# Reordering the first slice's sums, the stores of adj x, and the weight and feature loads of the first layer

## The chip, the cores and the metric

The kernel runs on one core of one Trainium2 chip, in one launch. The metric is the device time in microseconds (us). Three runs of the kernel before gave 1675.24, 1675.89 and 1678.59 us; their median is 1675.89 us.

## The reference

Four layers work on x of shape (8 batches, 2048 nodes, 64 features) with one dense adjacency matrix of 2048 x 2048, all in fp32. Each layer is `x = layernorm(x + f(x))` over the 64 features:

- layer 0: three Chebyshev terms x, A x and 2 A (A x) - x, each multiplied by weights of its own for every node (node embedding of 16 numbers times a weight bank of 16 x 3 x 64 x 64), plus a bias per node;
- layer 1: twice `relu((A x) W)`;
- layer 2: `x W_self + (A x) W_neighbor + b`;
- layer 3: x, A x, 2 A A x - x (twice, with the same matrix), concatenated and projected.

What takes the time is seven products of A with a 2048 x 512 matrix (all batches and features side by side) and the per-node projection of layer 0.

## The kernel before

**Fast products.** A product A b is computed by Strassen-Winograd on two levels: seven products of matrix halves instead of eight, A11, A12, A22, S1, S2, S3, S4, and each of these again as seven products of quarters. Left-hand sums such as S1 = A21 + A22 are made once, while A is first read, and stored in HBM as `comb` tensors; right-hand sums are made on VectorE (DVE) at each product.

**First product, by slices (L627 to L1005).** A x for layer 0 runs in four column slices, `ns` = 0 to 3. A slice is four chunks of 1 MB, `chunks[ns, j]`, loaded on the SyncE (SP) queue into a ring of four tiles (`slice_chunk`, L153) in the order j = 2, 3, 0, 1 (`AHEAD`). While TensorE (PE) multiplies a slice, the generator `prepare` (L627) makes the left-hand sums from the same chunks on DVE. Outer sums S1, S2, S4, S3 (`outer`, L657) go into tiles with the tag T, of which there are three; inner sums of four quarters each (`inner`, L644) go into tiles with the tag C, of which there are four. Each sum is stored to `comb` by GpSimd's DMA queue (POOL, `keep`, L640). All DVE instructions of `prepare` carry `keep_in_program_order`, so the places of its `yield`s fix the DVE order. Slice 0 is multiplied plainly in part (`plain_slice`, L846) and slices 1 to 3 by `fast_slice` (L880). In slice 1 the first inner sums that PE reads are those of A22, in a small two-level product (`two_level`, L802; matmuls of L816), and its chunks 0 and 1 are first read by the matmuls of L902 that make `pa` (L940).

**Queue of SP around slice 0.** After slice 0 the program issues the small weights (`load_weights`, L990), the four chunks of slice 1 (L991) and then the stores of adj x, transposed, to `t1T` (`keep_t1`, L767, called at L996). These instructions carry no fixed order, so the scheduler places them by its own estimate of when they are ready: in the kernel before, two chunks of slice 1, four stores, then six chunks. [...] a chunk's load waits until PE and DVE have read the tile it overwrites.

**Second product and the per-node projection (L1023 to L1097).** `product(1, ...)` (L212) goes through A11, S1, A12, S2, S4, S3, A22. Each takes seven loads of 1 MB (`load`, L196) into the same ring of four tiles, and each load feeds one group of eight matmuls (L273). A load is issued when PE has finished with the load four before it. Into this queue the kernel before also puts the loads of `xT` and `tT` for the projection (`fetch`, L1048): `tT` reads back what `keep_t1` stored. The projection's weights `wn` (1.5 MB) come on the POOL queue in two DMAs of 768 KB (L1032). `sum_wn` (L1034) combines and centers them in eight DVE instructions right after S1 (argument `between`, L419). The projection itself is `feature0` (L1055, matmuls of L1071), a job of a list (`pump`) that runs when `pump.run` is called: with `RUNS = {S2: NP, S3: NP}` four jobs after S2 and four after S3; the others run where all jobs are drained.

Of the kernel before, what the change touches and what calls it, by code (L numbers as in the profile page):

```python
# [11 lines left out]
ALU = mybir.AluOpType  # L12
# [6 lines left out]
GW = 512  # L19
# [3 lines left out]
A11, A12, A22, S1, S2, S3, S4 = range(7)  # L23
# [81 lines left out]
def kernel(  # L105
# [18 lines left out]
    nc = tc.nc  # L124
# [3 lines left out]
    F = b_l0.shape[1]  # L128
# [3 lines left out]
    NP = B // 2  # L132
    DH = D // 2
    RING = 4
# [10 lines left out]
    pump = Pump()  # L145
# [44 lines left out]


    loads = 0
    banks = 0
    p_mm2 = None

    def load(q, s):  # L196
        nonlocal loads
        loads += 1
        turn = loads % (RING + 3)
        pool = ring2 if ring2 is not None and turn >= RING else ring  # L200
        a = pool.tile([P, TG, TG, P], F32, tag="a", name="a")
        if q in (A11, A12, A22) and s < 4:
            i, j = {A11: (0, 0), A12: (0, 2), A22: (2, 2)}[q]
            fetched = nc.sync.dma_start(a, blocks[i + s // 2, j + s % 2])
        else:
            fetched = nc.sync.dma_start(a, comb[q][s].rearrange("p (n m c) -> p n m c", n=TG, m=TG))
        if ring2 is not None and loads <= RING + 3:

            tc.keep_in_program_order(fetched)
        return a  # L210

    def product(src, feature, between=None, rate=1, own=None, pin=False, runs=None, onto_slot=None, ends=False):  # L212
# [251 lines left out]
    class Norm:  # L464
# [18 lines left out]
        def center(self):  # L483
            sm = self.new("sm")
            nc.vector.tensor_reduce(sm, self.v, AX.X, ALU.add)
            nc.vector.scalar_tensor_tensor(self.v, self.wide(sm), -1.0 / F, self.v, ALU.mult, ALU.add)
# [91 lines left out]
    if True:  # L578
# [48 lines left out]
        def prepare(ns, ch, outers):  # L627

            ch = [c.rearrange("p m i n -> p i m n") for c in ch]

            def add(out, a, b, op=ALU.add):

                tc.keep_in_program_order(nc.vector.tensor_tensor(out, a, b, op))

            def kept(tag, shape, bufs):
                s = sums.tile([P, *shape, GW], F32, tag=tag, name="s" + ("i" if tag == "C" else "o"), bufs=bufs)
                n = "ab"[: len(shape)]
                return s, s.rearrange(f"p {' '.join(n)} (m n) -> p {' '.join(n)} m n", m=TG)

            def keep(q, s0, src):  # L640
                dst = comb[q][s0 : s0 + src.shape[1]].rearrange("s p (n c) -> p s n c", n=TG)
                nc.gpsimd.dma_start(dst[:, :, ns], src)

            def inner(q, q00, q01, q10, q11):  # L644
                flat, s = kept("C", (4,), 4)
                add(s[:, 0], q10, q11)
                add(s[:, 1], s[:, 0], q00, ALU.subtract)
                add(s[:, 2], q00, q10, ALU.subtract)
                add(s[:, 3], q01, s[:, 1], ALU.subtract)
                if q is not None:  # L650
                    keep(q, 4, flat)
                return flat

            def raw(I, J):
                return [ch[2 * J + b][:, 2 * I + a] for a in range(2) for b in range(2)]

            def outer(a, b, op):  # L657

                flat, s = kept("T", (2, 2), 3)
                for c in range(2):  # L660
                    add(s[:, :, c], a(c), b(c), op)
                return flat

            def rq(I, J):
                return lambda c: ch[2 * J + c][:, 2 * I : 2 * I + 2]

            def sq(s):
                return lambda c: s[:, :, c].rearrange("p a (m n) -> p a m n", m=TG)

            def put(q, s):  # L670
                flat = s.rearrange("p a b c -> p (a b) c")
                keep(q, 0, flat[:, :2])
                keep(q, 3, flat[:, 3:])
                inner(q, *(flat[:, k].rearrange("p (m n) -> p m n", m=TG) for k in range(4)))


            outers[A22] = inner(A22, *raw(1, 1))
            yield
            inner(A12, *raw(0, 1))
            if ns == 0:  # L680

                sums_of_blocks()
                outers[A11] = inner(A11, *raw(0, 0))
                outers[A21] = inner(None, *raw(1, 0))
            outers[S1] = s1 = outer(rq(1, 0), rq(1, 1), ALU.add)
            outers[S2] = s2 = outer(sq(s1), rq(0, 0), ALU.subtract)
            outers[S4] = s4 = outer(rq(0, 1), sq(s2), ALU.subtract)
            yield
            put(S1, s1)
            yield  # L690
            put(S2, s2)
            if ns:
                inner(A11, *raw(0, 0))
            yield
            outers[S3] = s3 = outer(rq(0, 0), rq(1, 0), ALU.subtract)
            yield
            put(S3, s3)
            put(S4, s4)
            yield

        with tc.tile_pool(name="p_n", bufs=4, space=PSUM) as p_n, tc.tile_pool(
# [63 lines left out]
                return p_n.tile([P, GW], F32, tag="mm", name="ps_n")  # L765

            def keep_t1(ns, p, hT):  # L767
                nc.sync.dma_start(
                    t1T[p].rearrange("f (i n c) -> f i n c", i=NG, n=TG)[:, :, ns],
                    hT.rearrange("f (i c) -> f i c", i=NG),  # L770
                )

            def new_h():
                return sums.tile([P, GW], F32, tag="t", name="hT", bufs=5)
# [195 lines left out]
            for ns in range(TG):  # L970
                ch = [chunks.pop((ns, j)) for j in range(NG)]
                if ns == 0:
                    outers = {}
# [50 lines left out]
        if True:  # L1024
# [3 lines left out]
            nc.gpsimd.dma_start(e_sb, emb)  # L1028

            wn = l0y.tile([P, 3, D, F], F32, tag="wn", name="wn")  # L1030
            for k in range(2):
                nc.gpsimd.dma_start(wn[k * F : (k + 1) * F], w_l0.rearrange("n i d o -> i n d o"))  # L1032

            def sum_wn():  # L1034
                pin = tc.keep_in_program_order
                pin(nc.vector.tensor_tensor(wn[:, 0], wn[:, 0], wn[:, 2], ALU.subtract))
                pin(nc.vector.tensor_scalar(wn[:, 2], wn[:, 2], 2.0, None, ALU.mult))
                for n in range(3):
                    center(wn[:, n], pin=pin)


            order = [
# [2 lines left out]
            ]  # L1045
            fetched = {}

            def fetch(k):  # L1048
                if k < len(order):
                    i, p = order[k]  # L1050
                    fetched[i, p] = [l0y.tile([P, GW], F32, tag=n, name=n, bufs=2) for n in ("xT", "tT")]
                    for tile_, src in zip(fetched[i, p], (xT, t1T)):
                        nc.sync.dma_start(tile_, src[p][:, ts(i, GW)])

            def feature0(g, p, hT):  # L1055
                if (g, p) == order[0]:
                    fetch(0)
                fetch(order.index((g, p)) + 1)
                terms = fetched.pop((g, p)) + [hT]
                for k in range(TG):  # L1060
                    t = g * TG + k
                    acc = xy[:, t, 0, ts(p, 2 * F)].rearrange("p (b f) -> p b f", f=F)


                    s = l0y.tile([P, DH, 2, F], F32, tag="s", name="s", bufs=2)
                    for h in range(2):
                        y = p_y.tile([P, 2, DH * F], F32, tag="y", name="y")
                        for n in range(3):
                            for b in range(2):
                                half = slice(b * F, (b + 1) * F)  # L1070
                                mm = nc.tensor.matmul(  # L1071
                                    y[:, b, :], terms[n][half, ts(k, P)],
                                    wn[half, n, h * DH : (h + 1) * DH, :],
                                    start=(n == 0), stop=(n == 2),
                                )
                                if n == b == h == 0:
                                    tc.keep_in_program_order(mm)
                        for d in range(DH):
                            e = e_sb[:, t, h * DH + d : h * DH + d + 1]
                            if h == 0:  # L1080
                                nc.vector.scalar_tensor_tensor(  # L1081
                                    acc, y[:, :, ts(d, F)], e, acc, ALU.mult, ALU.add
                                )
                            else:
                                nc.scalar.activation(s[:, d], y[:, :, ts(d, F)], AF.Copy, scale=e)  # L1085
                        if h == 0:
                            yield
                    n = DH // 2
                    while n:
                        nc.gpsimd.tensor_tensor(s[:, :n], s[:, :n], s[:, n : 2 * n], ALU.add)  # L1090
                        n //= 2
                    nc.gpsimd.tensor_tensor(acc, acc, s[:, 0], ALU.add)
                    yield


            RUNS = {S2: NP, S3: NP}
            product(1, then(feature0, 0, gap=4, pool_sq=True), sum_wn, rate=4, runs=RUNS)  # L1097


    late = p_z = None  # L1100
# [127 lines left out]
```

## Time and profile before

| what | value |
|---|---|
| median of three runs | 1675.89 us |
| the profiled execution's own time | 1674.71 us |
| its span, first to last instruction | 1672.9 us |
| around the span (difference) | 1.81 us |
| PE busy | 1657.7 us, 99% of the span |
| PE weight loads (beside PE) | 1061.1 us, 63% |
| DVE busy | 965.5 us, 58% |
| ScalarE (ACT) busy | 275.6 us, 16% |
| POOL busy | 246.9 us, 15% |
| mean granted PE clock | 0.997 |
| loads of A blocks and sums (`a<-comb`, `a<-in_blocks`) | 294 of 1 MB, median 4.8 us from issue to landing |
| chunks of slices (`a<-in_slices`, 1 MB) | 15, median 10.3 us to landing |
| stores `t1T<-hT` | 16 of 256 KB, median 6.5 us |
| `wn` on the POOL queue | 2 of 768 KB, median 16.9 us |

The profile is one execution. A page lists the busy time of each engine, the span in 40 slices of 41.8 us with the granted PE clock and the share of the 16 DMA engines, the chain of work that ended last, and groups of instructions by line. Other views of the same trace are used below: the waits by engine, the timeline of one engine in a window, and busy times by window. Times in them are microseconds from the start of the span. In a timeline line the columns are start, length, engine, line, operation, tiles, number of instructions, and in brackets the idle time ahead of it with what ended it. A line that merges several DMA issues covers the stretch from the first issue to the end of the last, waits included.

### The profile page before, as it was taken

To read this page: it belongs to the slowest core of one execution; us is meant where nothing else is said; L and a number is where in the kernel's file an instruction comes from. 1 tells how busy PE (TensorE), PEld (TensorE's weight loads), DVE (VectorE), ACT (ScalarE), POOL (GpSimd) and SP (SyncE) were. 2 spreads that over 40 slices of the span, in tenths; PEclk is the share of its full clock that TensorE was granted. 3 is DMA by queue.
4 is the path that set the end of the run, shared out by engine and by line. 5 is a ranking of instruction groups with operands and counts; after the bars stand their busy time and mean duration, and the time that the engine had idled before them with its cause. 6 is when DMAs were issued, how large, how long until landed. Compare 5 with 4: busy or idle time off the path is not lost.

```text
span 1672.9 us, 21268 instructions
## 1 busy us (share of the span) xinstructions
PE 1657.7 (99%) x8414; PEld 1061.1 (63%) x8414; DVE 965.5 (58%) x1737; ACT 275.6 (16%) x811; POOL 246.9 (15%) x334
## 2 busy tenths in 40 slices
PE   9999989999999999999999999999999999999998
PEld 5898844444444444444454455589998455569998
DVE  5986886457456456654434365873568344443657
ACT  0200100143143044430010011120001011100001
POOL 1221200155055056660000000000000000000000
PEclk9999999999999999999999999999999999999999
DMA  8899898503702800009877876667888866678995
GB/s 317 294 395 339 307 321 308 210 26 127 251 26 87 290 26 26 26 31 371 292 261 276 303 275 239 239 223 257 294 292 298 306 219 228 229 268 292 316 314 166
DMA packets 82436, 391.57 MB, mean 234 GB/s; under 512 B 8897, under 2 KB 25537, under 8 KB 42785
## 3 DMA queue, kind: packets, MB, share of 16 engines
q1 hardware_dynamic: 69104, 345.20, 58.5%
q0 software_dynamic: 11664, 43.65, 6.9%
q8 instruction: 67, 1.10, 0.3%
q10 hardware_dynamic: 1568, 1.35, 0.3%
q14 instruction: 33, 0.26, 0.0%
HBM read 339.85 MB, written 50.33 MB: 233 GB/s over the span
## 4 chain that ended last, share of the span: by engine, by line
PE 98%; DMA 2%; DVE 0%; issue 0%; SPq 0%; DVEq 0%
PE y L1071 20%; PE mmb L273 17%; PE mmc L273 12%; PE mma L273 11%; PE mmb L266 9%; PE ps_n L902 7%; PE mma L266 6%; PE mmc L266 6%; PE z L1123 3%; PE ps_i L816 2%; PE z L1152 2%; PE ps_n L856 2%; PE pt L1114 1%; DMA t1T<-hT 1%; DMA a<-in_slices 1%; DMA a<-comb 0%
## 5 line engine op out<-in xcount | busy, mean ns | idle before, releaser
L273 PE MATMUL mmb<-a,t 128*128 128x512 f32 x648 | 292.0, 593 | 0.0
L1081 DVE SCALAR_TENSOR_TENSOR xy<-y,e_sb,xy 128x128 f32<-128x128 f32 x512 | 179.6, 351 | 141.2 <-PE y L1071 125.3
L273 PEld LDWEIGHTS mmb<-a,t 128*128 128x128 f32 x648 | 121.7, 190 | 145.0 <-issue 143.5
L1090 POOL TENSOR_TENSOR s<-s 128x512 f32<-128x512 f32 (+2 forms) x192 | 157.1, 818 | 340.3 <-ACT s L1085 330.1
L1085 ACT ACTIVATE s<-y,e_sb 128x128 f32<-128x128 f32 x512 | 138.9, 382 | 231.9 <-PE y L1071 231.9
L224 DVE TENSOR_TENSOR u<-mmb,p 128x512 f32<-128x512 f32 x84 | 57.8, 688 | 177.5 <-PE mmb L273 121.1
L266 PE MATMUL mmb<-t,a 128*128 128x128 f32 x1344 | 157.0, 275 | 0.0
L266 PEld LDWEIGHTS mmb<-t,a 128*128 128x128 f32 x1344 | 153.5, 192 | 0.0
L1071 PE MATMUL y<-wn,xT 64*128 64x512 f32 x512 | 131.6, 591 | 0.0
L1071 PE MATMUL y<-wn,tT 64*128 64x512 f32 x512 | 131.2, 589 | 0.0
L1071 PE MATMUL y<-wn,C 64*128 64x512 f32 x512 | 131.2, 589 | 0.0
L273 PE MATMUL mma<-a,T 128*128 128x512 f32 x256 | 115.5, 594 | 0.0
L273 PE MATMUL mmc<-a,t 128*128 128x512 f32 x216 | 97.3, 593 | 0.0
L288 ACT COPY p<-mma 128x512 f32<-128x512 f32 x42 | 24.6, 586 | 411.9 <-PE mma L273 270.4
L1071 PEld LDWEIGHTS y<-wn,xT 64*128 64x128 f32 x512 | 49.4, 187 | 61.1 <-issue 60.6
L1071 PEld LDWEIGHTS y<-wn,tT 64*128 64x128 f32 x512 | 49.7, 187 | 60.2 <-issue 60.2
L1071 PEld LDWEIGHTS y<-wn,C 64*128 64x128 f32 x512 | 49.7, 187 | 60.2 <-issue 60.2
L273 PE MATMUL mma<-a,xy 128*128 128x512 f32 x192 | 86.7, 594 | 0.0
L273 PEld LDWEIGHTS mma<-a,T 128*128 128x128 f32 x256 | 47.7, 191 | 56.7 <-issue 56.4
L224 DVE TENSOR_TENSOR C<-mmc,C 128x512 f32<-128x512 f32 x48 | 33.2, 691 | 85.3 <-PE mmc L273 74.5
L273 PEld LDWEIGHTS mmc<-a,t 128*128 128x128 f32 x216 | 40.1, 191 | 45.4 <-issue 45.1
L1123 PEld LDWEIGHTS z<-wd,C 128*128 128x128 f32 x384 | 50.2, 192 | 21.7 <-issue 20.8
(157 smaller groups left out, 2115.3 us busy)
## 6 DMA issues: line engine op xcount, KB each, us to landing
a<-comb SPq DMA_DIRECT2D x240, 1024.0 KB, 4.8
a<-in_blocks SPq DMA_DIRECT2D x54, 1024.0 KB, 4.8
comb<-si POOLq DMA_DIRECT2D x28, 1024.0 KB, 9.8
a<-in_slices SPq DMA_DIRECT2D x15, 1024.0 KB, 10.3
comb<-so POOLq DMA_DIRECT2D x16, 512.0 KB, 11.6
comb<-so POOLq DMA_DIRECT2D x16, 256.0 KB, 11.4
t1T<-hT SPq DMA_DIRECT2D x16, 256.0 KB, 6.5
xT<-in_xT SPq DMA_DIRECT2D x16, 256.0 KB, 3.4
```

The lines of the kernel that those rows point to most:

```text
L224: nc.vector.tensor_tensor(out, a, b, op)
L266: nc.tensor.matmul(to, a[:, k, m, :], xb[:, m, :], start=(start and opens and m == 0), stop=(m == TG - 1), skip_group_check=True,)
L273: nc.tensor.matmul(ps, xb[:, m, :], a[:, :, m, :], start=(start and m == 0), stop=(m == TG - 1), skip_group_check=True,)
L816: nc.tensor.matmul(ps, x[:, m // 2, m % 2], s[n](m), start=(start and m == 0), stop=(m == TG - 1), skip_group_check=True,)
L856: mm = nc.tensor.matmul(ps[p], xcol(0, TG * j + m, p), ch[j][:, m], start=(n == 0 and m == 0), stop=(n == 1 and m == TG - 1), skip_group_c ...
L902: nc.tensor.matmul(ps[:, ts(p, GW // 2)], b(k, p), a(k // TG, k % TG), start=(start and p == k == 0), stop=(k == NT // 2 - 1), skip_group_ ...
L1071: mm = nc.tensor.matmul(y[:, b, :], terms[n][half, ts(k, P)], wn[half, n, h * DH : (h + 1) * DH, :], start=(n == 0), stop=(n == 2),)
L1081: nc.vector.scalar_tensor_tensor(acc, y[:, :, ts(d, F)], e, acc, ALU.mult, ALU.add)
L1085: nc.scalar.activation(s[:, d], y[:, :, ts(d, F)], AF.Copy, scale=e)
L1090: nc.gpsimd.tensor_tensor(s[:, :n], s[:, :n], s[:, n : 2 * n], ALU.add)
L1123: nc.tensor.matmul(z[:, k, :], aT[:, ts(k, P)], wd[:, w, :], start=(n == 0), stop=(n == len(terms) - 1),)
L1152: nc.tensor.matmul(z[n][:, k], xT[half, ts(k, P)], w[half], start=True, stop=True)
```

## The change

- **Third outer sum of slice 0.** S3 of slice 0 is made right after S4, ahead of the first `yield` that follows, in a tile of tag C instead of T. Its inner sums (`put(S3)`) then take the place where S3 itself was made. Slices 1 to 3 are as before.
- **Stores of slice 0.** The four `t1T` stores of slice 0 keep their program order, behind the four chunk loads of slice 1.
- **Weights `wn`.** Six DMAs of 256 KB on the SP queue, two for each of the three terms in the order 0, 2, 1, replace the two DMAs of 768 KB on POOL. `load` issues one behind its 6th, 9th, 12th, 15th, 18th and 21st load, in program order.
- **`sum_wn`.** It becomes a job of `pump`, the first one, and runs after A12 instead of after S1.
- **First `xT` and `tT`.** The first two pairs keep their program order: the first `feature0`, which runs after S2, issues both. In the built order they stand behind S2's last load.

In the built order of the changed kernel the instructions of PE and ACT are in the same order as before. On DVE, besides what is named, three sums of slice 1 (L924, L957, L958 of the kernel before) stand some ten small instructions later among the weight sums.

```diff
+    pieces = []
...
     def load(q, s):
...
+        if pieces and loads > RING and loads % 3 == 0:
+            tc.keep_in_program_order(pieces.pop(0)())
         return a
...
-            def outer(a, b, op):
-                flat, s = kept("T", (2, 2), 3)
+            def outer(a, b, op, tag="T"):
+                flat, s = kept(tag, (2, 2), 3 if tag == "T" else 4)
...
             outers[S4] = s4 = outer(rq(0, 1), sq(s2), ALU.subtract)
+            if ns == 0:
+                s3 = outer(rq(0, 0), rq(1, 0), ALU.subtract, "C")
             yield
             put(S1, s1)
             yield
             put(S2, s2)
             if ns:
                 inner(A11, *raw(0, 0))
             yield
-            outers[S3] = s3 = outer(rq(0, 0), rq(1, 0), ALU.subtract)
-            yield
+            if ns:
+                outers[S3] = s3 = outer(rq(0, 0), rq(1, 0), ALU.subtract)
+                yield
             put(S3, s3)
+            if ns == 0:
+                yield
             put(S4, s4)
...
             def keep_t1(ns, p, hT):
-                nc.sync.dma_start(
+                stored = nc.sync.dma_start(
...
+                if ns == 0:
+                    tc.keep_in_program_order(stored)
...
-            for k in range(2):
-                nc.gpsimd.dma_start(wn[k * F : (k + 1) * F], w_l0.rearrange("n i d o -> i n d o"))
+            pieces += [
+                lambda k=k, n=n: nc.sync.dma_start(wn[k * F : (k + 1) * F, n], w_l0[n])
+                for n in (0, 2, 1) for k in range(2)
+            ]
...
-            def fetch(k):
+            def fetch(k, pin=lambda inst: inst):
...
-                        nc.sync.dma_start(tile_, src[p][:, ts(i, GW)])
+                        pin(nc.sync.dma_start(tile_, src[p][:, ts(i, GW)]))
...
                 if (g, p) == order[0]:
-                    fetch(0)
-                fetch(order.index((g, p)) + 1)
+                    fetch(0, tc.keep_in_program_order)
+                    fetch(1, tc.keep_in_program_order)
+                else:
+                    fetch(order.index((g, p)) + 1)
...
-            RUNS = {S2: NP, S3: NP}
-            product(1, then(feature0, 0, gap=4, pool_sq=True), sum_wn, rate=4, runs=RUNS)
+            RUNS = {A12: 1, S2: NP, S3: NP}
+            product(1, then(feature0, 0, gap=4, pool_sq=True), lambda: pump.add(sum_wn()), rate=4, runs=RUNS)
```

More of the change, by code (lines that the diff above doesn't have):

```diff
@@ L1039, in sum_wn @@
                     center(wn[:, n], pin=pin)
+                yield
             order = [
```

## Prediction

> **What bounds the kernel now.** I read the page's busy slices first, then PE's waits, then the timelines of PE, SP and DVE around each wait.
>
> ```profile
> PE   9999989999999999999999999999999999999998
> ...
> PEclk9999999999999999999999999999999999999999
> DMA  8899898503702800009877876667888866678995
> ```
>
> PE is over 90% busy in 38 of 40 slices, at full clock; only the sixth (209 to 251 us) and the last show less. So a gain can come only from PE's waits. They are few:
>
> ```profile
> PE mmc L273 <- DMA a<-comb: 5.5, 1, 5.5
> PE ps_n L902 <- DMA a<-in_slices: 1.7, 1, 1.7
> PE rise L711 <- DVE zero L708: 1.1, 1, 1.1
> PE pt_n L458 <- ACT xy L459: 0.3, 1, 0.3
> ```
>
> The first two are near the edits; the start (1.1 us) and the chain behind the last matmul (the rest of the 15.2 us in which PE is idle) are untouched. Wait B, in the second product, on PE:
>
> ```profile
> 223.44 3.60 PE L273 MATMUL mmb<-a,C 128*128 128x512 f32 x8
> 232.56 5.40 PE L273 MATMUL mmc<-a,C 128*128 128x512 f32 x8 [5.53 <-DMA a<-comb]
> 237.80 3.60 PE L273 MATMUL mmb<-a,C 128*128 128x512 f32 x8
> ```
>
> Groups follow each other every 3.43 us (216.57, 220.00, 223.44). Unheld, this one begins at 226.87 and the next at 230.30, not 237.80: B costs 7.50 us, of which some 1.8 us is the group that ran 5.40 instead of 3.60 us. On SP, before it:
>
> ```profile
> 211.06 7.87 SPq L768 DMA_DIRECT2D t1T<-hT  x4
> 223.88 0.81 SPq L1053 DMA_DIRECT2D tT<-t1T  x2
> 224.79 0.38 SPq L206 DMA_DIRECT2D a<-comb  x1
> ```
>
> The load that PE waits for stands behind the two tT loads, and these wait for the stores that they read back to land (the chain gives 12.76 us from 211.06). It then needs 7.64 us. Wait A, in slice 1:
>
> ```profile
> 68.23 1.10 PE L816 MATMUL ps_i<-si,t 128*128 128x128 f32 x8
> ...
> 73.64 1.89 PE L902 MATMUL ps_n<-a,xy 128*128 128x256 f32 x8
> 77.23 2.00 PE L902 MATMUL ps_n<-a,xy 128*128 128x256 f32 x8 [1.70 <-DMA a<-in_slices]
> ```
>
> The second eight would follow 1.79 us after the first, at 75.43: A costs 1.80 us. Chunk 1 of slice 1 is issued at 66.66, behind the stores of slice 0, and lands at 77.19. DVE meanwhile:
>
> ```profile
> 40.15 0.55 DVE L831 TENSOR_TENSOR u<-u,part 128x384 f32<-128x384 f32 x1
> ...
> 63.44 2.35 DVE L633 TENSOR_TENSOR so<-a 128x1024 f32<-128x1024 f32 x2
> 65.71 0.69 DVE L633 TENSOR_TENSOR si<-a 128x512 f32<-128x512 f32 x1
> 66.43 0.69 DVE L633 TENSOR_TENSOR si<-si,a 128x512 f32<-128x512 f32 x1
> ```
>
> DVE is without a pause from 40 to 66 us (12.66 of 13.00 us busy between 53 and 66). The pair at 63.44 is S3 of slice 0; the lines after it are A22's inner sums of slice 1, of which PE reads the second at 68.23.
>
> [...] behind 5.53 us of idling the granted clock is 0.69 from 233 to 238 us, behind 1.70 us it is 1.00. [...] from 211 to 220 us POOL's queue takes 76.5% of the engines and SP's 27.0%, so SP's stores are slow while POOL's `comb` stores and `wn` drain. [...]
>
> **The change part by part.**
>
> *xT and tT behind S2's loads.* Load 5 of the second product then stands behind the four stores only. Its tile is free when group 1 ends (216.6); the stores are issued by 218.93 (211.06 + 7.87). So it is issued at 216.7 to 219.0 and lands, at its own 7.64 us, at 226.6 at worst; at the median of 4.8 us, at 221.5. PE wants it at 226.87. B goes, with the slow group: **-7.50 us**, at worst 0.1 to 1 us left. The two pairs now are issued when S2's third group has been read: 303.04 in the old time. They land 3.4 us later and the projection begins at 316.86: 10 us of cover. What is late next? DVE in A11 has, laid end to end from 227.7, the sum that frees the bank of S1's first group done 0.9 us before that group begins; nothing is late.
>
> *wn in six pieces on SP.* POOL loses two issues of 0.63 us. 1.5 MB and the two xT (0.5 MB) leave the crowded stretch 197 to 224 us, where SP's and POOL's transfers took up to 18 us to land; this is why I take the early end for load 5. The pieces then stand between loads 6 and 21. A load is issued three groups (10.3 us) before use and lands in 4.8: slack 5.5 us. A piece takes 256 KB by 385 GB/s (the rate from 230 to 240 us) = 0.68 us. From 238 to 260 us the engines are 0.86 busy at 302 GB/s; 1.5 MB in 56 us add 28 GB/s: 0.94. Cost 0; if the slack were gone, 0.7 us each, 4 us in all. What waits behind a piece on SP is the next load.
>
> *sum_wn after A12.* 1.22 + 0.69 + 3 x 1.21 + 3 x 1.22 = 9.2 us of DVE move from 269 to S2's stretch. Laid between S2's sums from 293.5 (old time), the sum that frees PE's second bank ends at 301.1 (needed 303.04), and the next at 304.7 (needed 306.47). The last piece is issued after load 21 (279.2), in place by 283 and used near 298. Cost 0, cover 1.8 us.
>
> *Slice 0's S3 early.* 2.27 us of DVE (63.44 to 65.71) go in at 40.15, and all DVE work up to 63.44 is 2.27 us later. PE is nearest in the part tiles (read until 52.1 then, overwritten by ACT at 52.75): 0.7 us of cover, so 0. At 65.71 four inner sums of S3 come first, 2.53 us (as A22's own, 65.71 to 68.24). A22's sums begin at 68.24 and the second ends at 69.65, where PE wants it at 68.23: a **new wait of 1.45 us**, as DVE has nothing to catch up on. The tile that S3 takes is free: the store of A22's sums, issued at 18.9, lands 10.3 us later. What the step buys is the early release of chunks 0 and 1.
>
> *Stores of slice 0 behind slice 1's loads.* Chunks 0 and 1 need their tiles read: by DVE (S3, now by 42.5) and PE (by 57.9). They are issued by 58, not 65.3 and 66.7, into a stretch in which the DMA engines are 41% busy (53 to 66 us), and land by 68.3 at the 10.3 us median. PE wants chunk 0 at 73.64 + 1.45 = 75.1. A goes: **-1.80 us**. Behind the stores on SP stand only slice 2's chunks, first issued at 81.9; the hT tiles are reused at 83.8. Both far off. L924, now behind some ten small weight sums, ends near 103.9 instead of 102.1, and PE overwrites the bank that it reads at 104.3: 0.4 us of cover.
>
> Sum: -7.50 - 1.80 + 1.45 = **-7.85 us**. Against the profiled execution: 1674.71 - 7.85 = 1666.9. That execution is 1.18 us under the median of the runs shown; from the median, 1675.89 - 7.85 = **1668.0 us**.
>
> **Rivals.**
> - *A22's wait doesn't come* (DVE catches up): -9.3 us, 1666.6 from the median, 1665.4 from the profiled execution. For it: A's two causes are both removed. Against: DVE has no gap from 40 to 66.
> - *The stores still hold load 5.* They stay ahead of it, and one took 5.12 us to issue. Gain 3.4 to 6.5 us, 1669.4 to 1672.5. Against: POOL's backlog is 2 MB, some 5 us, smaller then.
> - *Nothing measurable*: the freed time is lost again where DVE lags PE (cover 0.4 to 1.8 us at five places): within 3.4 us of 1675.9.
> - *Slower: the pieces of wn starve the loads.* If a piece held the queue at wn's old rate (16.9 us for 768 KB), it would cost 5.6 us. Loads 7 to 21 need 15 x 2.7 = 41 us of DMA in 51.5 us; spare 10.7 + slack 5.5 = 16.2. Six pieces, 33.6 us, make PE 17.4 us late: 1685.4. It loses from (16.2 + 7.85) / 6 = 4.0 us a piece on. Against: xT, also 256 KB, lands in 3.4 us.
>
> **Numbers.** Forecast (gain 6.5 to 8.5) 0.68; no new wait 0.10; stores hold load 5 0.09; nothing 0.07; slower 0.06. A measurement of this kernel can tell about 0.2% (3.4 us) from no change: faster 0.87, same 0.07, slower 0.06. The range goes from the no-wait case on the profiled base, 1665.4, to a gain of 4.4 from the median, 1671.5.
>
> **What would show it.** Right: PE's waits have no `a<-comb` line; clock 1.00 from 225 to 240 us; no `a<-in_slices` line, but one for L816's matmuls on DVE's `si` of about 1.4 us near 68. Wrong: a load wait in 225 to 300 us (stores or pieces), a wait at the first matmul of the projection on xT or wn, or one near 104 us.

## The result, and the profile after

Six runs of the changed kernel gave a median of 1667.22 us (1666.90 to 1668.05); the kernel before, beside it, gave 1675.32 us. The ratio is 0.9949, 95% interval 0.9936 to 0.9962: 8.10 us or 0.5% faster. 1668.0 was forecast. The profiled execution took 1667.24 us with a span of 1665.5 us, against 1674.71 and 1672.9 before: 7.47 and 7.4 us less.

The page of the kernel after, busy share and granted clock in 40 slices of the span:

```profile
PE   9999999999999999999999999999999999999998
...
PEclk9999999999999999999999999999999999999999
DMA  8998899504503600029878877667888856678894
```

The sixth slice, 8 before, is now 9: the hole that the forecast called B is filled. (The forecast's A is the wait for a chunk near 77 us.) All of PE's waits after (engine, tile, line, what ended the wait; us in total, times, longest):

```profile
PE rise L720 <- DVE zero L717: 1.1, 1, 1.1
PE ps_i L828 <- ACT part L832: 0.4, 1, 0.4
PE pt_n L461 <- ACT xy L462: 0.3, 1, 0.3
```

No load is left. The lines of the file have shifted: L273 is L276 now, L816 is L828, L902 is L914, L633 is L636. The timeline of PE at the two places:

```profile
68.18 1.06 PE L828 MATMUL ps_i<-a,xy 128*128 128x128 f32 x8
69.66 1.13 PE L828 MATMUL ps_i<-si,t 128*128 128x128 f32 x8 [0.42 <-ACT part L832]
...
75.10 3.62 PE L914 MATMUL ps_n<-a,xy 128*128 128x256 f32 x16
...
222.93 3.60 PE L276 MATMUL mmb<-a,C 128*128 128x512 f32 x8
226.36 3.60 PE L276 MATMUL mmc<-a,C 128*128 128x512 f32 x8
229.79 3.60 PE L276 MATMUL mmb<-a,C 128*128 128x512 f32 x8
```

The sixteen matmuls on slice 1's chunks run in one piece (x16 in 3.62 us, where before there were two lots of eight with 1.70 us between), and the groups of the second product follow each other every 3.43 us. From 230 us on PE is 8.01 us earlier than before, and it is 8.00 us earlier at the last matmul (1654.66 against 1662.66). Behind the start of the last group this execution took 0.6 us longer, so the span gained 7.4.

SP's timeline after shows why:

```profile
39.30 19.04 SPq L158 DMA_DIRECT2D a<-in_slices  x4
58.43 8.90 SPq L777 DMA_DIRECT2D t1T<-hT  x4
...
210.55 2.81 SPq L777 DMA_DIRECT2D t1T<-hT  x4
216.25 0.34 SPq L207 DMA_DIRECT2D a<-comb  x1
```

All four chunks of slice 1 are out before the stores of slice 0. In the second product the load behind the stores is issued at 216.25 us, not at 224.79: it waits for its tile alone, lands 4.8 us later, at 221.05, and PE wants it at 226.36. DVE around the new wait:

```profile
40.27 2.36 DVE L636 TENSOR_TENSOR si<-a 128x1024 f32<-128x1024 f32 x2
...
65.57 2.61 DVE L636 TENSOR_TENSOR si<-si 128x512 f32<-128x512 f32 x4
68.10 0.69 DVE L636 TENSOR_TENSOR si<-a 128x512 f32<-128x512 f32 x1
68.83 0.69 DVE L636 TENSOR_TENSOR si<-si,a 128x512 f32<-128x512 f32 x1
```

S3's outer sums stand at 40.27, its four inner sums at 65.57, and the sum that A22 needs ends at 69.52 (68.83 + 0.69). PE starts on it at 69.66. The waits view puts PE's 0.42 us down to ACT, whose copy ends at 69.59. But in e4_s3_inner_late and r1_changed_again (below) the same matmuls start at 69.00 and 69.37, before that copy does (69.25 and 69.49), so they do not wait for it. What is left is DVE's sum, and e4 shows it.

### The profile page after: what moved, and what is told of

The parts are those of the page before. It is cut to its first block, busy times and chain, and to the rows that moved or that the text cites. A ratio compares the mean times of both kernels' runs of the same rounds, so it can differ in the third digit from the quotient of the medians.

```text
span 1665.5 us, 21273 instructions
## 1 busy us (share of the span) xinstructions
PE 1656.5 (99%) x8414; PEld 1060.5 (64%) x8414; DVE 965.7 (58%) x1737; ACT 276.2 (17%) x811; POOL 245.6 (15%) x332
## 4 chain that ended last, share of the span: by engine, by line
PE 99%; DVE 0%; ACT 0%; issue 0%; DVEq 0%; ACTq 0%
PE y L1089 20%; PE mmb L276 17%; PE mma L276 12%; PE mmc L276 12%; PE mmb L269 9%; PE ps_n L914 7%; PE mma L269 6%; PE mmc L269 6%; PE ps_i L828 3%; PE z L1141 3%; PE z L1170 2%; PE ps_n L868 2%; PE pt L1132 1%; PE pt_n L461 0%; PE rise L720 0%; PE mmd L269 0%
## 5 line engine op out<-in xcount | busy, mean ns | idle before, releaser
L276 PE MATMUL mmb<-a,t 128*128 128x512 f32 x648 | 292.0, 593 | 0.0
L276 PEld LDWEIGHTS mmb<-a,t 128*128 128x128 f32 x648 | 121.5, 190 | 145.3 <-issue 143.3
L276 PE MATMUL mma<-a,T 128*128 128x512 f32 x256 | 115.5, 594 | 0.0
L276 PE MATMUL mmc<-a,t 128*128 128x512 f32 x216 | 97.3, 592 | 0.0
L276 PE MATMUL mma<-a,xy 128*128 128x512 f32 x192 | 86.7, 593 | 0.0
L276 PEld LDWEIGHTS mma<-a,T 128*128 128x128 f32 x256 | 47.6, 190 | 56.8 <-issue 56.5
L276 PEld LDWEIGHTS mmc<-a,t 128*128 128x128 f32 x216 | 40.0, 190 | 45.4 <-issue 45.2
```

What stands on the lines that cost most here:

```text
L276: nc.tensor.matmul(ps, xb[:, m, :], a[:, :, m, :], start=(start and m == 0), stop=(m == TG - 1), skip_group_check=True,)
```

## The experiments

**Theory**: each of the two load waits is a load that stands behind slow stores on SP's queue; B goes because the `tT` loads, which wait for stores to land, are moved, A because the chunks go ahead of the stores; the early S3 has a price on DVE. **Rivals**: B goes because `wn` or `xT` leave the crowded stretch (bytes, not order); the early release of the tiles by S3 is what removes A; the new wait doesn't come from S3's inner sums; pieces of `wn` nearly starve the loads. Differences are of medians, against the kernel before on the same chip; the ratio has its 95% interval.

| run | what is in it | median us | difference us | ratio |
|---|---|---|---|---|
| e1_slice0 | S3 early + stores pinned | 1675.34 | -0.53 | 0.9999 (0.9991 to 1.0007) |
| e2_queue | all of the change but those two | 1668.21 | -7.66 | 0.9955 (0.9942 to 0.9967) |
| e3_fetch | `xT`, `tT` pinned alone | 1667.64 | -8.23 | 0.9952 (0.9940 to 0.9965) |
| e4_s3_inner_late | all, S3's inner sums after A22's | 1666.58 | -9.29 | 0.9946 (0.9934 to 0.9959) |
| r1_changed_again | the changed kernel once more | 1666.97 | -8.76 | 0.9947 (0.9934 to 0.9959) |
| e5_min_best | e4 without the moves of `wn`, `sum_wn` | 1666.08 | -9.65 | 0.9947 (0.9934 to 0.9961) |
| e6_pieces_x4 | changed, 24 transfers for 6 | 1668.08 | -7.65 | 0.9953 (0.9939 to 0.9967) |
| e7_pieces_x8 | changed, 48 transfers for 6 | 1684.52 | +8.79 | 1.0050 (1.0036 to 1.0063) |
| e8_stores_alone | stores pinned alone | 1674.15 | -1.62 | 0.9989 (0.9980 to 0.9997) |
| e9_s3_alone | S3 early alone | 1675.90 | +0.13 | 1.0001 (0.9992 to 1.0009) |
| e10_xT_alone | `xT` pinned alone | 1674.02 | -1.75 | 0.9990 (0.9982 to 0.9999) |
| e11_stores_fetch | e3 + e8 | 1665.64 | -10.06 | 0.9941 (0.9927 to 0.9955) |

### The two halves of the change

e1_slice0 is the kernel before with the early S3 and the pinned stores; e2_queue is the changed kernel with these two undone.

> The kernel before with the slice-0 edits alone (S3 early in a C tile, stores of slice 0 behind slice 1's chunks); the second product as before. My theory: the wait on a<-in_slices (1.7 us, near 77) goes, and a wait of L816's matmuls on A22's inner sums near 68 to 69.7 takes its place, so PE is 0.3 to 0.5 us earlier from 80 us on; the wait on a<-comb at 227 stays at its 7.5 us of cost. Time: 0.3 to 0.5 us under the kernel before. Rival (DVE catches up, no new wait): 1.8 to 2.0 us under it.

> The changed kernel with the slice-0 edits undone: only the second product's edits (xT and tT behind S2's loads, wn in six pieces on SP, sum_wn after A12). My theory: the wait on a<-comb goes with the slow group behind it, 7.5 us under the kernel before; the wait on a<-in_slices near 77 stays at 1.7 us. Rival (the two parts depend on each other): less than 6.5 or more than 8.5 us.

PE's timeline in e1_slice0:

```profile
71.17 1.13 PE L823 MATMUL ps_i<-si,t 128*128 128x128 f32 x8 [1.91 <-DVE si L633]
...
234.26 5.11 PE L273 MATMUL mmc<-a,C 128*128 128x512 f32 x8 [6.23 <-DMA a<-comb]
```

In slice 0 the load wait of 1.70 us became a DVE wait of 1.91 us, and nothing measurable was won; B stayed. In e2_queue B is gone and PE (`ps_n L905`) waits for a chunk again, 1.3 us. Nearly the whole gain is in the second half.

### What removes B: order or bytes

e3_fetch pins `xT` and `tT` and leaves `wn` and `sum_wn` as before. e10_xT_alone pins `xT` only:

```diff
-            def fetch(k):
+            def fetch(k, pin=lambda inst: inst):
...
-                        nc.sync.dma_start(tile_, src[p][:, ts(i, GW)])
+                        inst = nc.sync.dma_start(tile_, src[p][:, ts(i, GW)])
+                        if src is xT:
+                            pin(inst)
...
-                    fetch(0)
-                fetch(order.index((g, p)) + 1)
+                    fetch(0, tc.keep_in_program_order)
+                    fetch(1, tc.keep_in_program_order)
+                else:
+                    fetch(order.index((g, p)) + 1)
```

(e3_fetch has it without the condition.)

> The kernel before with one edit: the first two pairs of xT and tT behind S2's loads; wn stays on POOL's queue in two DMAs and sum_wn behind S1. Theory 1 (the wait for the stores to land, at the head of SP's queue, is the whole of it): load 5 is issued at about 219, lands in time or at most 1 us late, 6.5 to 7.5 us under the kernel before. Theory 2 (the crowd of wn on POOL's queue holds it as well): the stores still take 7.9 us to issue, load 5 lands at 228 to 231, a wait of 1 to 4 us is left, 3.5 to 6.5 us under the kernel before.

> The kernel before with the first two xT loads moved behind S2's loads, and the tT loads left ahead of load 5. Theory 1 (load 5 stands behind the tT loads, which wait for the stores to land): the wait for a<-comb stays, 4 to 6.2 us, less only by what 0.5 MB less in the queue ahead of it saves (0.5 MB at 302 to 384 GB/s is 1.4 to 1.7 us at most); 0 to 2 us under the kernel before. Rival (the 0.5 MB of xT in the crowded stretch is what makes it late): the wait goes and 7 us or more are gained.

SP's timeline in e3_fetch:

```profile
211.06 6.42 SPq L768 DMA_DIRECT2D t1T<-hT  x4
217.57 0.99 SPq L206 DMA_DIRECT2D a<-comb  x1
```

and in e10_xT_alone:

```profile
211.09 6.43 SPq L768 DMA_DIRECT2D t1T<-hT  x4
222.47 0.87 SPq L1053 DMA_DIRECT2D tT<-t1T  x2
223.43 0.38 SPq L206 DMA_DIRECT2D a<-comb  x1
```

The stores are issued alike (6.4 us). With `tT` in between, the load goes out 5.9 us later. The 5 us from the last issue of a store (217.5) to 222.47 is SP standing at `tT` until the stores have landed, as the chain of the kernel before has it:

```profile
211.06 12.76 DMA t1T<-hT
...
223.88 0.33 SPq L1053
```

The store issued at 211.06 lands at 223.82 there, and `tT`, which reads it back, goes out at 223.88. So the order makes the wait: without the 0.5 MB of `xT` ahead of it the wait is still 4.23 us. The median of e10_xT_alone is 1.75 us better, where the expectation had at most 2; its traced execution won nothing (last section). The wait at `tT` also held a load that had nothing to do with it: behind `tT` that went out at 223.43, and without it at 217.57.

The bytes decide how much room is left. PE's timeline in e3_fetch:

```profile
227.08 3.67 PE L273 MATMUL mmc<-a,C 128*128 128x512 f32 x8
```

In e3_fetch PE's group starts at 227.08 instead of the 226.87 of the forecast. In the trace of before PE started 0.13 us after the landing (232.43, 232.56), so by my estimate the load lands at 226.95 here, 9.4 us after its issue at 217.57. In the changed kernel, without `wn` on POOL's queue, it takes 4.8 us. Moving `xT` and `tT` is just enough. What moving `wn` adds is at most 0.3 us of PE in the traces (the next group starts at 230.59, not 230.30) and some 5 us of margin, and in the medians nothing (e3_fetch won 8.23 us with POOL's `wn` untouched, e2_queue 7.66). The change of queue also moves the bytes to a later time (the first piece goes out at 220.12 us in the changed kernel, the two transfers of before at 197.9 and 204.9); no run here measures the rate of the two queues by itself. No run moves `tT` without `xT`. The stores' issue takes 6.43 us in e10_xT_alone and 7.87 before, so by my estimate the load would be some 1.5 us late with `xT` left in place (issued 1.44 us later than in e3_fetch, with the same 9.4 us to land).

### What removes A, and what S3 costs

e8_stores_alone has one edit, e9_s3_alone has the S3 part of the change's diff:

```diff
-                nc.sync.dma_start(
+                stored = nc.sync.dma_start(
...
+                if ns == 0:
+                    tc.keep_in_program_order(stored)
```

> The kernel before with slice 0's stores pinned behind slice 1's loads, and nothing else. Theory (chunk 1 of slice 1 is late because its tile is read by S3's outer sums until 65.7 us and because the stores go first; either alone holds it): the chunks are issued near 65.7 instead of 65.3 and 66.7, and PE's wait for a<-in_slices near 77 us stays at 0.7 to 1.7 us. Rival (the stores alone are the cause): the wait is gone. The wait for a<-comb stays at 5.5 to 6.2 us in both cases. Time within 1.5 us of the kernel before.

> The kernel before with S3's outer sums of slice 0 early in the tile of inner sums, and nothing else; its stores stay free, and the order on SP is two chunks, two stores, two chunks. Theory: the tiles of chunks 0 and 1 are released by 58 us, so both are issued near 54 and 58 and the wait for a<-in_slices goes, or shrinks below 0.5 us; in its place A22's wait on the vector engine's si of 0 to 1.9 us, as in the run of slice 0 alone. Rival (both halves are needed): the wait for a<-in_slices stays over 1 us. Time within 1.5 us of the kernel before.

PE's waits in e8_stores_alone:

```profile
PE mmc L273 <- DMA a<-comb: 5.6, 1, 5.6
PE rise L711 <- DVE zero L708: 1.1, 1, 1.1
```

and SP's timeline there:

```profile
64.75 1.46 SPq L158 DMA_DIRECT2D a<-in_slices  x2
66.27 1.35 SPq L768 DMA_DIRECT2D t1T<-hT  x2
```

What I expected of e8_stores_alone fell, and its rival held: the stores' place alone removes A, with S3 still late. Chunk 1 goes out at 65.88 us, 0.78 earlier than the 66.66 of before (1.46 us cover two issues, each of 0.33), but what counts is the flight: the two chunks need 5.4 and 8.5 us to land, against 7.6 and 10.5 before, now that the stores' 1 MB is behind them. Chunk 1 has landed by 74.4 at the latest, and PE wants it at 75.98 (74.19 + 1.79). In e9_s3_alone A is gone too, by the early release (all four chunks are out by 57.5 us), but A22 waits for DVE and the sum is +0.13 us:

```profile
70.14 1.13 PE L821 MATMUL ps_i<-si,t 128*128 128x128 f32 x8 [1.73 <-DVE si L633]
```

Either half removes A; only S3 has a price.

e4_s3_inner_late keeps S3 early and puts its inner sums behind A22's:

```diff
-            put(S3, s3)
             if ns == 0:
                 yield
+            put(S3, s3)
             put(S4, s4)
```

> The changed kernel with the four inner sums of slice 0's S3 moved behind the four of slice 1's A22 (one yield moved), all else the same. My theory of the new wait: those four sums, 2.53 us, are what keeps PE waiting at 68 to 69.7 us; here A22's second sum ends at 67.1 and nothing waits, so PE is 1.4 us earlier than in the changed kernel less what its own later start costs: 0.6 to 1.5 us under the changed kernel, 8.7 to 9.6 under the kernel before. Rival (DVE's 2.27 us of S3 itself keeps PE): no gain over the changed kernel.

> The changed kernel once more, as the base of the two runs with more copies. Theory: 7.5 to 8.7 us under the kernel before (it measured 8.1). PE's waits: no load; the first matmul on A22's second inner sum starts near 69.6 us whatever PE's own start is, since the vector engine's chain sets it; if the first matmul of this run starts earlier than 5.92 us, the wait shown there is longer than 0.42 by the same amount. Rival (the wait is PE's own late start): it would go with an early start.

PE's timeline in e4_s3_inner_late:

```profile
69.00 1.10 PE L828 MATMUL ps_i<-si,t 128*128 128x128 f32 x8
```

No wait is left, so the 2.5 us of inner sums, and not the 2.3 us of S3 itself at 40 us, make it. In r1_changed_again the same matmuls started at 69.37 and no wait is shown: DVE was 0.3 us earlier than in the first profile (its sum ended at 69.22), and PE arrived at 69.24 by itself. So the 69.6 "whatever PE's own start is" that I expected does not hold: DVE's own times move too. In the six traces that have the changed order (after, r1, e1, e6, e7, e9) S3's outer sums start at 40.00 to 41.81 us, the sum that A22 needs ends 29.2 us later in each, and the matmuls start at 69.37 to 71.17. How long PE stands idle, 0 to 1.9 us, depends on both its own time and DVE's.

### The minimal version, and the best

> Only what the runs so far found to earn something: xT and tT pinned behind S2's loads, stores of slice 0 pinned, S3's outer sums early, its inner sums behind A22's of slice 1; wn's two transfers stay on POOL's queue and its weight sums stay where they were. Theory 1 (SP's wait for the stores to land is all of wait B; moving wn earns nothing): 9.0 to 9.5 us under the kernel before, the same as the kernel with S3's inner sums late (9.29), within 0.5 us. Rival (wn's move earns something once the vector engine's wait is gone): 1 us or more slower than that kernel, with a wait for a<-comb or a late bank release in A11.

> The two steps that earned something when alone, put together, and nothing else of the change: slice 0's stores pinned behind slice 1's loads, and xT and tT pinned behind S2's loads; S3 stays late, wn stays on POOL. Theory (the two waits are separate, and S3's early step is not needed for either): 8.23 + 1.62 = 9.85 us under the kernel before, 9.0 to 10.0, so 0.5 to 2 us under the changed kernel; PE's waits have neither a load of either product nor one for A22's si. Rival (S3's early step is needed once the queue is free, or the two gains overlap): a wait for a<-in_slices of over 0.7 us is back near 77 us, or the gain stays at 8.3 or less.

e5_min_best gave 9.65 us and shows no wait but `rise` and `pt_n`: again `wn` earns nothing that the medians show. (Its load is 0.2 us late, as in e3_fetch.) Since e8 shows S3's step to be unneeded, e11_stores_fetch leaves it out. PE's waits in e11_stores_fetch:

```profile
PE rise L711 <- DVE zero L708: 1.1, 1, 1.1
PE pt_n L458 <- ACT xy L459: 0.3, 1, 0.3
```

It won 10.06 us, against an expected 9.85, the sum of e3 and e8: two separate waits. All five of its runs (1665.40 to 1665.86) are under the fastest of the eleven of the changed kernel (1666.90). They are from another chip, and the intervals of the two ratios overlap, so how much better it is stays open. It has two of the five parts of the change.

Its trace began the first product at 5.04 us, as the kernel before did (5.02), so the two can be laid side by side without the start. PE's timeline in e11_stores_fetch:

```profile
73.64 3.62 PE L904 MATMUL ps_n<-a,xy 128*128 128x256 f32 x16
...
221.47 3.60 PE L273 MATMUL mmb<-a,C 128*128 128x512 f32 x8
...
228.47 3.60 PE L273 MATMUL mmb<-a,C 128*128 128x512 f32 x8
```

At 73.64 us the two are level. Behind A PE is 1.97 us earlier than before (221.47 against 223.44), and behind B 9.33 us (228.47 against 237.80). The forecast's terms without the new wait are 1.80 + 7.50 = 9.30 (A gave 0.17 more, and the load is 0.1 us late here).

### How near the pieces of wn are to starving the loads

e6_pieces_x4 and e7_pieces_x8 put three and seven unused copies of 256 KB, from HBM to HBM, ahead of each piece:

```diff
...
+            def piece(n, k):
+                for r in range(7):
+                    tc.keep_in_program_order(nc.sync.dma_start(spare[n, k, r], w_l0[n]))
+                return nc.sync.dma_start(wn[k * F : (k + 1) * F, n], w_l0[n])
...
```

(This is e7_pieces_x8; e6_pieces_x4 has `range(3)`.)

> The changed kernel with three unused 256 KB copies from memory to memory ahead of each piece of wn on SP, so 24 transfers in place of 6 between the loads; the copies are work that is left out of no output. If a transfer of 256 KB costs the queue 0.68 us (the forecast's price): 24 x 0.68 = 16.3 us against 16.2 us spare, so 0 to 1 us slower than the changed kernel, and no more than short load waits. Rival (a transfer holds the queue far longer, 2 us or more): 24 x 2 = 48 us, some 30 us slower.

> The same with seven copies ahead of each piece: 48 transfers. At the forecast's price of 0.68 us: 32.6 us against 16.2 spare, about 16 us slower than the changed kernel, with waits of PE for a<-in_blocks and a<-comb between 235 and 290 us. If DMA engines have more room than the forecast took, or if copies from memory to memory run faster: under 8 us slower. Rival (2 us or more each): 80 us or more slower.

PE's waits in e7_pieces_x8:

```profile
PE mmb L276 <- DVE C L227: 6.2, 1, 6.2
PE mmc L276 <- DMA a<-comb: 3.7, 2, 3.5
PE mmb L276 <- DMA a<-comb: 1.9, 1, 1.9
...
PE mmb L276 <- DVE u L227: 1.0, 1, 1.0
```

Against r1_changed_again e6 lost 1.11 us and e7 lost 17.55; 0 to 1 and about 16 were expected. In e6 PE waits for no load, though the engines' share is 0.99 to 1.02 from 225 to 295 us (0.85 to 0.97 in the changed kernel): so the spare time may just be used up there. What e6 lost is `mmb` waiting 1.0 us for the sum that frees its bank: the weight sums of `sum_wn` stood in one block ahead of it there. In e7 the engines' share is 0.99 to 1.03, and the next 24 transfers cost 16.44 us (1684.52 - 1668.08), 0.69 us each; the forecast had 0.68. Two cautions. Some 5 us of that is PE at half clock behind the waits (granted clock 0.50 from 244 to 250 and from 289 to 294 us, groups of 5.61 and 6.72 us instead of 3.60). And 6.2 us is a wait for DVE: the scheduler had put the bank's sum behind three long operations there (at 245.99, in the changed kernel at 237.75). That it only fills time in which PE would have waited for loads anyway is argued from the engines' share, not shown. The rival of 2 us or more a transfer, which would have cost 30 us in e6 and 80 us in e7, is refuted.

## Why the prediction was right, point by point

- **B, -7.50 us: right in cause and size.** On PE: 8.01 us earlier behind the place less 0.51 us before it is 7.50. By medians, with the step alone (e3), 8.23. The load was issued at 216.25 us, 216.76 in the old time; 216.7 to 219.0 was forecast. It landed in 4.8 us because `wn` had left POOL's queue, which is what the forecast took the early end for; in e3, where `wn` stayed, it was 0.2 us late, within the forecast's worst case.
- **A, -1.80 us: size 0.2 us short, one half of the reason wrong.** It measured 1.97 us in e11. The forecast had it that the S3 step "buys" the early release of the chunks. e8 removed A without S3, for 1.62 us.
- **New wait, +1.45 us: right in cause, its exact size in part luck.** It is there, on DVE's `si`, because of S3's inner sums. (The forecast's own times, 69.65 less 68.23, give 1.42.) In the profile after only 0.42 us shows as idle time. This execution began its first product at 5.92 us instead of 5.02, so PE itself came at 69.07 (68.18 + 0.89), 0.84 later than in the profile of before. The matmuls start at 69.66, 1.43 us later than the old 68.23, of which the late start covers 0.84. In the six traces with this order they start 1.14 to 2.94 us later than 68.23. So the sign that the forecast named, a wait of about 1.4 us, did not show as such. The rival without this wait had -9.3 us; the runs that take its cause away gave 9.29 (e4), 9.65 (e5) and 10.06 (e11).
- **wn's pieces, 0 us: right.** The price of 0.68 us a piece fits e6 and e7, with the two cautions above.
- **sum_wn, 0 us: right.** The sum that frees PE's bank ends at 293.46 in the new time, 301.5 in the old; 301.1 was forecast. PE's group starts at 295.03, so the cover is 1.6 us, where 1.8 was forecast. In e6, where the weight sums stand in one block ahead of that sum, it is used up.
- **What the sum was not sure of**: at the last group PE is 8.00 us earlier in the trace, -7.85 was forecast; A's 0.17 us accounts for that. The medians gained 8.10 and 8.76 us. Some of the rest may be B, which costs 7.46 to 7.91 us in the five traces that have it (before, e1, e8, e9, e10), and 7.50 in the profile of before; and starts differ by 0.9 us between executions. How the rest divides stays open.

## What to carry to other kernels

On a queue that keeps its order, as SP's did here (5 us at `tT` held the load behind it), look for the instruction that waits longest for something other than its neighbours do, and count what stands behind it: moving the loads that read back a store, with the `xT` loads that go with them, was worth 8 us, while the 1.5 MB of weights that were moved as well won nothing that the medians show, only room. When several edits aim at one wait, try each alone: here either removed the wait, and one of them brought an extra wait on DVE. And work that is moved earlier can bring the work that follows from it forward as well, as S3 did with its inner sums; the new place of these in an engine's order needs pricing, too.

## What was not expected of the hardware

In the four traces read for it (before, e1, e7, e10) the stretch at half clock that goes with a stall of 3.5 to 6.2 us has one length, 6.8 us, so a shorter stall can cost as much as a longer one. Busy times by window in e10_xT_alone (PE, its weight loads, DVE, ACT, POOL, then granted clock, share of the DMA engines, GB/s):

```profile
229.00:230.00 1.00, 0.00 (x0) 0.00 (x0) 1.00 (x2) 0.00 (x0) 0.00 (x0) 1.00 0.99 418
230.00:231.00 1.00, 0.00 (x0) 0.00 (x0) 1.00 (x2) 0.00 (x0) 0.00 (x0) 0.74 1.05 442
...
237.00:238.00 1.00, 1.00 (x3) 0.38 (x2) 0.01 (x1) 0.00 (x0) 0.00 (x0) 0.85 0.22 90
```

A mean of 0.74 in a window of 1 us at clocks of 1.00 and 0.50 puts the drop at 230.48, and 0.85 puts the return at 237.30: 6.82 us. By the same reading it is 6.84 us in the kernel before (229.22 to 236.06), 6.82 in e1_slice0 (230.34 to 237.16) and 6.82 for both stalls of e7_pieces_x8 that have one (from 243.78 and from 288.16). It begins 2.2 us after PE stops in the kernel before (227.04 to 229.22) and 3.4 us after in e10_xT_alone (227.07 to 230.48); the ends of PE's work are modelled. Nor did one length of work bring the clock back: PE had been at work for 3.5 us in the kernel before, 2.9 in e1_slice0 (234.26 to 237.16) and 6.0 in e10_xT_alone. What sets the start and the length of the stretch is not shown. In two traces the part of the stretch behind the stall cost about half its length: in the kernel before 3.50 us of it lie there and the group ran 1.80 us longer, in e10_xT_alone 6.00 us and 3.05; the part within the stall cost nothing more. PE's timeline in e10_xT_alone:

```profile
231.30 6.65 PE L273 MATMUL mmc<-a,C 128*128 128x512 f32 x8 [4.23 <-DMA a<-comb]
237.79 3.60 PE L273 MATMUL mmb<-a,C 128*128 128x512 f32 x8
```

The wait was 1.30 us shorter than the 5.53 of before, but the group behind it took 6.65 us instead of 5.40, and the next one began at 237.79 in place of 237.80: in this execution the shorter stall won nothing. That other executions, where the drop falls otherwise, make up the 1.75 us of the medians is possible and not shown.
